# A two-layer graph network on one core: when GpSimd issues its adding transfers, and what the last batch does once attention is over

## The chip, the cores and the metric

The kernel runs on one core of a Trainium2 chip. The metric is the time of one execution on the device, in microseconds (us), as the median of the runs. A core has five engines with a queue of instructions each: TensorE (PE, with its weight loads as PEld), VectorE (DVE), ScalarE (ACT), GpSimd (POOL) and SyncE (SP, which here only issues transfers), and 16 DMA engines that move data for all of them.

## The reference

There are B = 16 batches of N = 1024 nodes with D = 256 features, and a 0/1 matrix `adj` of 1024 x 1024 per batch. Cut to what matters, each batch computes this:

```python
h = relu(layernorm(x))
v = layernorm(h) * gamma1 + beta1              # 8 heads of 32, queries = keys = values
h = h + softmax(where(adj > 0, v v^T / sqrt(32), -inf)) v            # per head
x = x + h + gelu(layernorm2(h) @ W1 + b1) @ W2 + b2                  # W1: 256 x 1024
f = relu(layernorm(x))
hh = f @ W
e = leaky_relu(hh a_1 (as a row) + hh a_2 + (hh a_12) hh^T)
x = x + elu(f @ W_1 + (softmax(where(adj > 0, e, -9e15)) f) @ W_2)
```

The kernel takes softmax without subtracting a row's maximum. At the end it tests that this was harmless: that all denominators of the second softmax (`dens`) lie in a range, and that the sum of squares of the folded weights is under 1e4. If not, a general program (`general_path`) would compute everything again. The test's result is `redo`.

## The kernel before

`fast_path` writes out all 16 batches as one straight program. Nothing loops on the chip; the order is decided when the program is written.

**Attention of a batch** (`attention`, stream A) has 32 units: 2 halves of the queries (`qh`), 2 groups of 4 heads (`g`), 8 tiles of 128 keys (`kt`). A unit makes scores `s` on TensorE (L937), adds the mask on VectorE into two tiles `e`, one for each pair of heads (L958; the first pair is "half 0", the second "half 1"), and takes their exponential on ScalarE (L961). One unit later `weigh` multiplies them with the values into `o` (L974). For the denominators the exponentials of the 8 key tiles are added up: the two tiles of `kt` = 0 are the sums `acc`, and each later tile is added to its `acc` by a transfer that adds on its way (L999, `add_up`), issued on GpSimd's queue. A transfer adds to what the last transfer of the same half has left, so it waits until that one has landed. In batch 0 only the even `kt` are added in this way. After the eighth tile, `go_on` takes a finished group in three steps, one per unit: `weigh`, then a step in which it lies in `summed`, then `total`, which multiplies `acc` with ones (`den`, L888). `finish` follows as an entry of the list `turns`: it transposes denominators and sums (`ptds`, `ptos`, L909), divides, and adds to `h`. The tiles `e` come from a pool of five (`ep`).

**The rest of a batch** (`rest`, stream B) runs beside the attention of the next batch: four chunks of 256 nodes go through `expand` (`ph`, W1, gelu) and `contract` (`po`, W2), then the second layer: `project` (`puT`), `values` (`pg`), `weights` (`lg`), `attend` (`pf`, `pa`). Ahead of each stage lies a normalization: `norm_stats` takes mean and variance on VectorE (L705 to L708) and the power -1/2 on GpSimd (`rs`, L710); VectorE then scales (`y`, `ft`, L714); TensorE transposes (`pty` L1095, `ptf` L1171). The last two `attend` of a batch (`tail`) are run inside the `rest` of the next batch; after the last batch they end the program.

**The order** comes from a planner. Each stream is a Python generator that yields a place (batch number plus fraction) after each piece, and the stream with the lowest place goes next. A piece of stream B moves its place on by its estimated time over 134 us; a unit of attention moves stream A's by 1/32. Two side lists shift work: `turns` holds transposes that wait for the next unit of attention (`ask` appends, `make_turns` empties), and `defer(us, f)` holds work that is written out when the planner's `clock` has advanced by `us`. The clock is a plan, not a measured time: `go_on` adds 2.0 per unit, most pieces of stream B add 1.75. Each engine keeps the order in which its instructions were written out. GpSimd's queue so holds, in one order, the adding transfers, the powers `rs`, the products for the values (`nrm`, `va`, L780 and L781), the sums of the residuals (`h`, `xb`, L1067 and L1068) and the addition of `finish` (L916).

**The end.** After the last unit `close_attention` calls `go_on` four times to empty those three steps, with places between 16 and 16.05. It then sets `quarters[0] = False`: from there matmuls of the rest are written as whole 128-column ones (L567) and not as four of 32 columns (L570). Once stream A has ended, `turns` is emptied only when stream B says that it can't go on (`wait_for`, which yields `0.0, None`). After the last output the test is made: L1433 to L1441 reduce `dens` and the folded weights to `seen` on VectorE, a matmul with ones adds over the partitions (`pn`, L1443), and L1445 to L1448 make `redo`, which all engines load.

The lines that set when a transfer is written out, and what empties the list at the end:

```python
        def add_up(qh, g, kt, es):                                   # L995
            if b == 0 and kt % 2:
                return
            for e, a in zip(es, sums[g, qh]):
                nc.gpsimd.dma_start(a, e, accum_op=ALU.add)
...
                defer(1.5, lambda u=u, es=es: add_up(*u, es))        # L1011
...
                    if places[1] is None:                            # L1380
                        make_turns()
```

Of the kernel before, what the change touches and what calls it, by code (L numbers as in the profile page):

```python
# [16 lines left out]
P = 128  # L17
# [476 lines left out]
def fast_path(  # L494
# [158 lines left out]
    nc.gpsimd.memset(gw[:, :, D + 1 : D + 2], 1.0)  # L653
    dens = const.tile([P, B * NT], F32, name="dens")

    def setup():
        wl, wa, wT, wb = (lp1.tile([P, DC, D], F32, tag="e1", name=f"stage_{i}") for i in range(4))
        weights_to_load.extend([(wl, W), (wa, a_12)])  # L660
        for t, src in rows_to_load:
            nc.sync.dma_start(t, src)
        for t, src in weights_to_load:
            nc.scalar.dma_start(t, src.rearrange("(c p) n -> p c n", p=P))
        yield

        for oc in range(DC):
            pt = ps_tile([P, DC, P], f"p_wT_{oc}")
            for ic in range(DC):
                nc.tensor.transpose(pt[:, ic, :], wl[:, ic, oc * P : (oc + 1) * P], ident)  # L670
            nc.scalar.copy(wT[:, oc, :], pt.rearrange("p c q -> p (c q)"))
        clock[0] += 0.5
        yield

        def product(dst, lhs, rhs, n, name):

            for oc in range(DC):
                pp = ps_tile([P, n], f"p_{name}_{oc}")
                for kc in range(DC):
                    matmul(  # L680
                        pp,
                        lhs[:, kc, oc * P : (oc + 1) * P],
                        rhs[:, kc, :n],
                        start=(kc == 0),
                        stop=(kc == DC - 1),
                    )
                nc.scalar.copy(dst[:, oc, :], pp)

        product(wb, wa, wT, D, "wb")
        clock[0] += 1.7  # L690
        yield
        product(wm, wT, wb, D, "wm")
        product(w_a2.unsqueeze(2), wT, a2c.unsqueeze(2), 1, "w_a2")
        product(wo2[:, :, D : D + 1], wT, a1c.unsqueeze(2), 1, "w_a1")
        nc.gpsimd.memset(wo2[:, :, D + 1 : D + 2], 0.0)
        clock[0] += 2.0
        yield

    def norm_stats(srcs, name):
# [218 lines left out]
    def attention(b, st):  # L918
        va, kT = st["va"], st["kT"]


        def scores(qh, g, kt):
            qs = slice(qh * QW, (qh + 1) * QW)
            sc = [
                psc.tile([P, 2, QW], F32, tag=f"sc{i}", name=f"s_{b}_{g}_{qh}_{kt}_{i}") for i in range(2)
            ]

            by_pe = 2 if b == 0 else 0
            if by_pe:
                for j in range(by_pe):  # L930
                    matmul(
                        sc[j // 2][:, j % 2, :], ident8, st[qh][:, kt // 2, :, kt % 2], start=True, stop=False
                    )
                clock[0] += 0.45
            for j in range(GH):
                r = slice(j * HD, (j + 1) * HD)
                nc.tensor.matmul(  # L937
                    sc[j // 2][:, j % 2, :],
                    kT[r, g, kt * P : (kt + 1) * P],
                    kT[r, g, qs],  # L940
                    start=j >= by_pe,
                    stop=True,
                )
            mb = st[qh][:, kt // 2, :, kt % 2].unsqueeze(1).to_broadcast([P, 2, QW])
            es = []
            if b == 0 and kt % 2:

                odd = midp.tile([P, 2, 2, QW], F32, tag="mid", name=f"odd_{g}_{qh}_{kt}")
            for i in range(2):
                if b == 0 and kt % 2:  # L950
                    e = odd[:, i]
                elif kt == 0:
                    e = accp.tile([P, 2, QW], F32, tag=f"acc{i}", name=f"acc_{b}_{g}_{qh}_{i}")
                else:
                    e = ep.tile([P, 2, QW], F32, tag="e", name=f"e_{b}_{g}_{qh}_{kt}_{i}")
                masked = sc[i]
                if 2 * i >= by_pe:
                    nc.vector.tensor_tensor(e, masked, mb, op=ALU.add)  # L958
                    masked = e
                es.append(e)  # L960
                weights = lambda e=e, masked=masked: nc.scalar.activation(e, masked, AF.Exp, scale=SCALE)  # L961
                if i == 0:
                    weights()
            return es, weights

        acc = {}


        def weigh(qh, g, kt, es):
            if kt == 0:  # L970
                acc[g, qh] = pso.tile([P, QW], F32, tag="o", name=f"o_{b}_{g}_{qh}")
            o = acc[g, qh]
            for j in range(GH):
                nc.tensor.matmul(  # L974
                    o[j * HD : (j + 1) * HD, :],
                    va[:, kt, (g * GH + j) * HD : (g * GH + j + 1) * HD],
                    es[j // 2][:, j % 2, :],
                    start=(kt == 0),
                    stop=(kt == NT - 1),
                )  # L980
            if b == 0 and kt % 2:

                if kt > 1:
                    for n, (e, w) in enumerate(zip(es, odds[g, qh])):
                        defer(1.0 + 2.5 * n, lambda e=e, w=w: nc.vector.tensor_add(e, e, w))
                odds[g, qh] = es
            if kt == NT - 1:
                c = tmpp.tile([P, QW], F32, tag="w2", bufs=3, name=f"os_{b}_{g}_{qh}")
                nc.vector.tensor_copy(c, o)
                weighed.append((b, qh, g, c, [s[g, qh] for s in (sums, odds) if s]))  # L990

        sums, odds = {}, {}


        def add_up(qh, g, kt, es):  # L995
            if b == 0 and kt % 2:
                return
            for e, a in zip(es, sums[g, qh]):
                nc.gpsimd.dma_start(a, e, accum_op=ALU.add)  # L999

        units = [(qh, g, kt) for qh in range(NQH) for g in range(NG) for kt in range(NT)]
        for u in units:
            make_turns()
            es, rest_of_weights = scores(*u)
            go_on()
            rest_of_weights()
            qh, g, kt = u
            if kt == 0:
                sums[g, qh] = es
            else:  # L1010
                defer(1.5, lambda u=u, es=es: add_up(*u, es))  # L1011
            scored.append((weigh, (*u, es)))
            yield

# [24 lines left out]
    def prepare(b, st, c):  # L1039
# [11 lines left out]

        st["y", c] = None, defer(5.0, apply)

    def rest(b, st, tails):

        h = hs[b]
# [16 lines left out]
        def ask(turn, c):  # L1073

            def f():
                clock[0] += 0.5
                turn(c)
                turned.add((turn, c))
            turns.append((1, f))

        def wait_for(turn, c):
            while (turn, c) not in turned:
# [160 lines left out]
        def attend(t, es):  # L1243
# [27 lines left out]
                nc.sync.dma_start(rows(out, b, t), z)  # L1271

            defer(1.0, lambda: nc.scalar.activation(en, z, AF.Exp, bias=ones[:, 0:1]))
            defer(6.0, store)
            yield 1.75, True

# [70 lines left out]
            before = es  # L1347

        def tail():
            for i in range(TPC):  # L1350
                yield from attend((NCH - 1) * TPC + i, before)

# [13 lines left out]
    def stream_a():  # L1366
        for b in range(B):
            yield from spread(attention(b, states[b]), 32, b, b + 1)
        yield from spread(close_attention(), 4, B, B + 0.05)

    def stream_b():
        for b in range(B):
# [55 lines left out]

    good = ep.tile([P, B * NT], F32, tag="e", name="good")
    nc.vector.tensor_scalar(good, dens, DEN_MIN, None, op0=ALU.is_ge)  # L1433
    nc.vector.scalar_tensor_tensor(good, dens, DEN_MAX, good, op0=ALU.is_le, op1=ALU.mult)
    seen = smallp.tile([P, 2], F32, tag="seen", name="seen")
    nc.vector.tensor_reduce(seen[:, 0:1], good, axis=mybir.AxisListType.X, op=ALU.add)
    sq = ep.tile([P, DC * D + 2 * DC], F32, tag="e", name="sq")
    for src, o, n in ((wm, 0, DC * D), (w_a2, DC * D, DC), (wo2[:, :, D], DC * D + DC, DC)):
        src = src.rearrange("p c n -> p (c n)") if len(src.shape) == 3 else src
        nc.vector.tensor_tensor(sq[:, o : o + n], src, src, op=ALU.mult)  # L1440
    nc.vector.tensor_reduce(seen[:, 1:2], sq, axis=mybir.AxisListType.X, op=ALU.add)  # L1441
    pn = ps_tile([1, 2], "pn")
    nc.tensor.matmul(pn, ones[:, 0:1], seen, start=True, stop=True)  # L1443
    fit = smallp.tile([1, 2], F32, tag="fit", name="fit")
    nc.vector.tensor_scalar(fit[:, 0:1], pn[:, 0:1], float(P * B * NT), None, op0=ALU.is_ge)  # L1445
    nc.vector.tensor_scalar(fit[:, 1:2], pn[:, 1:2], 1.0e4, None, op0=ALU.is_le)
    nc.vector.tensor_mul(fit[:, 0:1], fit[:, 0:1], fit[:, 1:2])
    nc.vector.tensor_scalar(redo, fit[:, 0:1], -1.0, 1.0, op0=ALU.mult, op1=ALU.add)  # L1448

    last = {}  # L1450
# [74 lines left out]
```

## Time and profile before

| what | value |
|---|---|
| time, median of 3 runs | 3539.3 us (3532.96 to 3562.22) |
| the profiled run | 3545.29 us, span of its instructions 3543.5 us |
| TensorE busy | 3458.9 us (98%) |
| VectorE / ScalarE / GpSimd busy | 77% / 52% / 40% |
| adding transfers | 864 of 512 KB, 453.04 MB, 69.8% of the DMA engines' span |

A line of a group or of the timeline names engine, source line and operation, then "out<-in" by the program's own names; "x8" is a number of instructions, and "[1.53 <-DVE xb L1149]" says that the engine stood idle for 1.53 us ahead of it and that this instruction ended the wait. The records of matmuls overlap, and their ends are modelled, so that TensorE's busy share also covers short gaps. "PEclk" is the clock granted to TensorE as a share of the full one.

### The profile page before, as it was taken

What the parts mean: (1) busy time and instruction counts of PE and PEld (TensorE: products, weight loads), DVE (VectorE), ACT (ScalarE), POOL (GpSimd) and SP (SyncE); (2) the same over time, 40 slices, a digit from 0 to 9 for tenths busy, and PEclk for the clock granted to TensorE, in tenths of its full rate; (3) what the DMA queues carried; (4) which work ended last, traced back from release to release, by engine and by line L of the source; (5) the groups of instructions that cost most, each with busy time, mean ns of one, the idle gap of its engine ahead of it and who ended that gap; (6) DMA issues with size and microseconds to landing.
All of it is one profiled execution on the core that took longest, in us unless ns stands there. A gap on an engine that the chain in (4) does not pass through costs nothing.

```text
span 3543.5 us, 107149 instructions
## 1 busy us (share of the span) xinstructions
PE 3458.9 (98%) x46494; PEld 1674.4 (47%) x46494; DVE 2733.4 (77%) x5189; ACT 1854.2 (52%) x2184; POOL 1414.0 (40%) x1708
## 2 busy tenths in 40 slices
PE   6999999999999999999999999999999999999998
PEld 2344444444444444444444444444444444444467
DVE  6878787787787877878787787877878778787744
ACT  5655554455555555555555555555555555555522
POOL 3543443434434344453434434344343444533220
PEclk9999999999999999999999999999999999999999
DMA  7799989999899998989989988998999989899710
GB/s 186 157 177 176 188 164 175 169 180 179 160 188 171 185 186 165 186 167 182 188 171 183 170 181 180 185 181 157 187 168 182 188 161 188 170 182 179 153 40 14
DMA packets 281859, 597.79 MB, mean 169 GB/s; under 512 B 94882, under 2 KB 130084, under 8 KB 281380
## 3 DMA queue, kind: packets, MB, share of 16 engines
q0 software_dynamic: 124416, 453.04, 69.8%
q1 hardware_dynamic: 154276, 134.41, 15.1%
q8 instruction: 367, 6.01, 0.7%
q10 hardware_dynamic: 2688, 3.41, 0.3%
q14 instruction: 112, 0.92, 0.1%
HBM read 104.21 MB, written 16.78 MB: 34 GB/s over the span
## 4 chain that ended last, share of the span: by engine, by line
PE 73%; DMA 13%; DVE 5%; issue 5%; POOL 2%; ACT 2%; ACTq 0%; SPq 0%; POOLq 0%; DVEq 0%
PE s L937 12%; DMA acc<-e 12%; PE pa L570 11%; PE o L974 10%; PE lg L570 10%; PE ph L570 9%; PE po L570 7%; PE pf L570 3%; PE pg L570 2%; DVE e L958 2%; PE puT L570 2%; PE den L888 1%; PE ptk L788 1%; PE pa L567 1%; POOL acc L999 1%
## 5 line engine op out<-in xcount | busy, mean ns | idle before, releaser
L961 ACT ACTIVATE e<-e 128x1024 f32<-128x1024 f32 x852 | 895.4, 1057 | 1011.8 <-DVE e L958 776.3
L999 POOL DMA_DIRECT2D acc<-e x864 | 759.2, 885 | 1664.4 <-ACT e L961 710.3
L958 DVE TENSOR_TENSOR e<-s,mk 128x1024 f32<-128x1024 f32 x852 | 1002.5, 1216 | 183.6 <-PE s L937 150.1
L937 PE MATMUL s<-kT 32*128 32x512 f32 x4096 | 596.4, 644 | 4.8 <-DVE e L958 2.7
L974 PE MATMUL o<-e,va 128*32 128x512 f32 x3456 | 463.2, 606 | 2.1 <-ACT e L961 2.1
L570 PE MATMUL ph<-yT,w 128*32 128x256 f32 x7808 | 450.0, 380 | 0.0
L570 PE MATMUL lg<-fT,uT 128*32 128x256 f32 x7680 | 448.6, 380 | 0.0
L570 PE MATMUL pa<-gw,e 128*32 128x258 f32 x7552 | 446.5, 380 | 0.0
L570 PE MATMUL po<-w,hid 128*32 128x256 f32 x7680 | 439.0, 379 | 0.0
L570 PEld LDWEIGHTS ph<-yT,w 128*32 128x32 f32 x7808 | 254.7, 110 | 215.6 <-issue 54.1
L570 PEld LDWEIGHTS lg<-fT,uT 128*32 128x32 f32 x7680 | 249.7, 110 | 211.1 <-issue 44.9
L570 PEld LDWEIGHTS po<-w,hid 128*32 128x32 f32 x7680 | 250.0, 110 | 209.2 <-issue 59.1
L570 PEld LDWEIGHTS pa<-gw,e 128*32 128x32 f32 x7552 | 244.7, 110 | 210.3 <-issue 56.8
L1219 DVE SCALAR_TENSOR_TENSOR e<-lg,gw,mk 128x256 f32<-128x256 f32 x512 | 223.0, 477 | 73.8 <-PE lg L570 63.4
L1225 ACT ACTIVATE e<-e,shift 128x512 f32<-128x512 f32 x256 | 182.2, 717 | 176.3 <-DVE e L1224 110.4
L1122 DVE TENSOR_TENSOR hid<-ph,b1c 128x512 f32<-128x512 f32 x256 | 175.1, 686 | 95.3 <-PE ph L570 81.4
L937 PEld LDWEIGHTS s<-kT 32*128 32x128 f32 x4096 | 163.8, 184 | 165.7 <-issue 114.2
L974 PEld LDWEIGHTS o<-e,va 128*32 128x32 f32 x3456 | 68.8, 108 | 332.5 <-issue 191.9
L961 ACT ACTIVATE acc<-acc 128x1024 f32<-128x1024 f32 x124 | 130.5, 1057 | 125.6 <-DVE acc L958 121.5
L1224 DVE SCALAR_TENSOR_TENSOR e<-e 128x512 f32<-128x512 f32 x256 | 188.7, 737 | 8.8
L958 DVE TENSOR_TENSOR acc<-s,mk 128x1024 f32<-128x1024 f32 x124 | 146.0, 1217 | 16.6 <-PE s L937 16.2
L1129 ACT ACTIVATE hid<-hid 128x2048 f32<-128x2048 f32 x64 | 122.3, 1911 | 36.0 <-DVE hid L1122 35.3
(144 smaller groups left out, 3822.7 us busy)
## 6 DMA issues: line engine op xcount, KB each, us to landing
acc<-e POOLq DMA_DIRECT2D x864, 512.0 KB, 6.0
adj<-in_adj_dram SPq DMA_DIRECT2D x248, 256.0 KB, 5.2
h<-in_x_dram SPq DMA_DIRECT2D x64, 256.0 KB, 6.3
xb<-in_x_dram SPq DMA_DIRECT2D x128, 128.0 KB, 5.3
out_dram<-z SPq DMA_DIRECT2D x128, 128.0 KB, 3.7
adj<-in_adj_dram SPq DMA_DIRECT2D x4, 512.0 KB, 6.7
mk<-mq SPq DMA_TRANSPOSE x128, 6.5
w<-in_L_gnn_W_dram ACTq DMA_DIRECT2D x2, 1024.0 KB
```

The source lines that it names most:

```text
L567: nc.tensor.matmul(out, lhsT, rhs, start=start, stop=stop)
L570: nc.tensor.matmul(out[c : c + HD], lhsT[:, c : c + HD], rhs, start=start, stop=stop)
L937: nc.tensor.matmul(sc[j // 2][:, j % 2, :], kT[r, g, kt * P : (kt + 1) * P], kT[r, g, qs], start=j >= by_pe, stop=True,)
L958: nc.vector.tensor_tensor(e, masked, mb, op=ALU.add)
L961: weights = lambda e=e, masked=masked: nc.scalar.activation(e, masked, AF.Exp, scale=SCALE)
L974: nc.tensor.matmul(o[j * HD : (j + 1) * HD, :], va[:, kt, (g * GH + j) * HD : (g * GH + j + 1) * HD], es[j // 2][:, j % 2, :], start=(kt = ...
L999: nc.gpsimd.dma_start(a, e, accum_op=ALU.add)
L1122: nc.vector.tensor_tensor(hid[:, f0 : f0 + 2, :], ph, b1c[:, f0 : f0 + 2].unsqueeze(2).to_broadcast([P, 2, CW]), op=ALU.add,)
L1129: return hid, defer(1.0, lambda: nc.scalar.activation(hid, hid, AF.Gelu))
L1219: nc.vector.scalar_tensor_tensor(e[:, j, :], lg[:, j, :], gw[:, kt, D : D + 1], st[c // 2][:, kt // 2, qs, kt % 2], op0=ALU.add, op1=ALU.add,)
L1224: nc.vector.scalar_tensor_tensor(e, e, ALPHA, e, op0=ALU.mult, op1=ALU.max)
L1225: ready = defer(2.5, lambda: nc.scalar.activation(e, e, AF.Exp, bias=shift))
```

## The change

There are four edits, of which the fourth has three places.

1. The adding transfers of a unit are written out one by one: half 0 after 2.0 on the planner's clock, half 1 after 3.5. Before, both came after 1.5.
2. `ask` empties `turns` at once when `quarters[0]` is False, that is, after the end of attention.
3. `close_attention` spreads its four calls over places 16 to 16.1.
4. The sums of the last test: those over the folded weights move into a fifth piece of `setup` in batch 0; those over `dens` are taken in two parts, columns 0 to 125 at the start of the last `tail` and the last two columns right after the last denominator is read. `seen` has four columns, and one more reduction adds them in pairs.

```diff
+    seen = const.tile([P, 4], F32, name="seen")
...
+        sq = lp1.tile([P, DC * D], F32, tag="e1", name="sq")
+        few = smallp.tile([P, 2 * DC], F32, tag="few", bufs=1, name="few")
+        wmf = wm.rearrange("p c n -> p (c n)")
+        nc.vector.tensor_tensor(sq, wmf, wmf, op=ALU.mult)
+        nc.vector.tensor_tensor(few[:, :DC], w_a2, w_a2, op=ALU.mult)
+        nc.vector.tensor_tensor(few[:, DC:], wo2[:, :, D], wo2[:, :, D], op=ALU.mult)
+        nc.vector.tensor_reduce(seen[:, 0:1], sq, axis=mybir.AxisListType.X, op=ALU.add)
+        nc.vector.tensor_reduce(seen[:, 1:2], few, axis=mybir.AxisListType.X, op=ALU.add)
...
-        def add_up(qh, g, kt, es):
+        def add_up(qh, g, kt, e, i):
             if b == 0 and kt % 2:
                 return
-            for e, a in zip(es, sums[g, qh]):
-                nc.gpsimd.dma_start(a, e, accum_op=ALU.add)
+            nc.gpsimd.dma_start(sums[g, qh][i], e, accum_op=ALU.add)
...
-                defer(1.5, lambda u=u, es=es: add_up(*u, es))
+                for i in range(2):
+                    defer(2.0 + 1.5 * i, lambda u=u, e=es[i], i=i: add_up(*u, e, i))
...
+    def count_fit(lo, hi, i):
+        good = smallp.tile([P, hi - lo], F32, tag=f"good{i}", bufs=1, name=f"good_{i}")
+        nc.vector.tensor_scalar(good, dens[:, lo:hi], DEN_MIN, None, op0=ALU.is_ge)
+        nc.vector.scalar_tensor_tensor(good, dens[:, lo:hi], DEN_MAX, good, op0=ALU.is_le, op1=ALU.mult)
+        nc.vector.tensor_reduce(seen[:, i : i + 1], good, axis=mybir.AxisListType.X, op=ALU.add)
...
             turns.append((1, f))
+            if not quarters[0]:
+                make_turns()
...
+            if n == B * NT - 1:
+                count_fit(n + 1 - TPC, n + 1, 3)
...
         def tail():
+            if b == B - 1:
+                count_fit(0, B * NT - TPC, 2)
...
-        yield from spread(close_attention(), 4, B, B + 0.05)
+        yield from spread(close_attention(), 4, B, B + .1)
...
-    good = ep.tile([P, B * NT], F32, tag="e", name="good")
-    nc.vector.tensor_scalar(good, dens, DEN_MIN, None, op0=ALU.is_ge)
...
-    pn = ps_tile([1, 2], "pn")
+    pn = ps_tile([1, 4], "pn")
     nc.tensor.matmul(pn, ones[:, 0:1], seen, start=True, stop=True)
     fit = smallp.tile([1, 2], F32, tag="fit", name="fit")
...
+    nc.vector.tensor_reduce(fit, pn.rearrange("o (i j) -> o i j", j=2), axis=mybir.AxisListType.X, op=ALU.add)
+    nc.vector.tensor_scalar(fit[:, 0:1], fit[:, 0:1], 1.0e4, None, op0=ALU.is_le)
+    nc.vector.scalar_tensor_tensor(
+        fit[:, 0:1], fit[:, 1:2], float(P * B * NT), fit[:, 0:1], op0=ALU.is_ge, op1=ALU.mult
+    )
     nc.vector.tensor_scalar(redo, fit[:, 0:1], -1.0, 1.0, op0=ALU.mult, op1=ALU.add)
```

More of the change, by code (lines that the diff above doesn't have):

```diff
@@ L696, in setup @@
         clock[0] += 2.0
+        yield
+        sq = lp1.tile([P, DC * D], F32, tag="e1", name="sq")
[6 more added lines that the diff above has]
+        nc.vector.tensor_reduce(seen[:, 1:2], few, axis=mybir.AxisListType.X, op=ALU.add)
         yield
@@ L1427, in fast_path @@
     run_deferred()
-    good = ep.tile([P, B * NT], F32, tag="e", name="good")
-    nc.vector.tensor_scalar(good, dens, DEN_MIN, None, op0=ALU.is_ge)
[L1434 to L1441, printed above, removed]
-    pn = ps_tile([1, 2], "pn")
+    pn = ps_tile([1, 4], "pn")
     nc.tensor.matmul(pn, ones[:, 0:1], seen, start=True, stop=True)
     fit = smallp.tile([1, 2], F32, tag="fit", name="fit")
-    nc.vector.tensor_scalar(fit[:, 0:1], pn[:, 0:1], float(P * B * NT), None, op0=ALU.is_ge)
-    nc.vector.tensor_scalar(fit[:, 1:2], pn[:, 1:2], 1.0e4, None, op0=ALU.is_le)
-    nc.vector.tensor_mul(fit[:, 0:1], fit[:, 0:1], fit[:, 1:2])
+    nc.vector.tensor_reduce(fit, pn.rearrange("o (i j) -> o i j", j=2), axis=mybir.AxisListType.X, op=ALU.add)
[3 more added lines that the diff above has]
+    )
     nc.vector.tensor_scalar(redo, fit[:, 0:1], -1.0, 1.0, op0=ALU.mult, op1=ALU.add)
```

## The prediction

> **What bounds the kernel now.** I read the page's head first, then its chain of work, then the windows by stage, the waits, and at last the timeline where TensorE waited.
>
> ```profile
> span 3543.5 us, 107149 instructions
> PE 3458.9 (98%) x46494; PEld 1674.4 (47%) x46494; DVE 2733.4 (77%) x5189; ACT 1854.2 (52%) x2184; POOL 1414.0 (40%) x1708
> ...
> PE 73%; DMA 13%; DVE 5%; issue 5%; POOL 2%; ACT 2%; ACTq 0%; SPq 0%; POOLq 0%; DVEq 0%
> ...
> acc<-e POOLq DMA_DIRECT2D x864, 512.0 KB, 6.0
> ```
>
> TensorE bounds it: busy for 98%, 73% of the chain. The chain's second part, 13%, is the adding transfers; each takes 6.0 us to land, in a unit of attention of about 6.7 us (215 us a batch over 32 units). They are the near second. So only what makes TensorE wait can be won, and the windows say how much there is (columns: length, busy PE, PEld, DVE, ACT, POOL, granted clock, DMA share, GB/s):
>
> ```profile
> 0.00:230.00 230.00, 192.62 (x2080) 73.34 (x2084) 173.63 (x311) 124.77 (x142) 101.79 (x131) 1.00 0.81 175
> 230.00:3360.00 3130.00, 3103.24 (x43480) 1472.77 (x43476) 2471.45 (x4670) 1681.60 (x1978) 1290.92 (x1551) 1.00 0.90 176
> 3360.00:3543.50 183.50, 163.06 (x946) 128.32 (x938) 88.29 (x210) 47.87 (x66) 21.26 (x28) 0.96 0.14 32
> 569.70:576.60 6.90, 6.90 (x42) 2.28 (x44) 4.93 (x10) 3.98 (x5) 1.72 (x2) 0.51 1.03 220
> 3378.90:3385.70 6.80, 5.61 (x52) 2.36 (x54) 0.23 (x1) 0.58 (x1) 0.00 (x0) 0.50 0.02 4
> ```
>
> In 15 batches' body TensorE is idle for 3130.0 - 3103.2 = 26.8 us, at the end for 183.5 - 163.1 = 20.4 us. The last two rows show a second price: after a wait of 2.7 us the clock is at half for some 6.9 us, which costs about 3.4 us more. Two more such stretches, of 3.4 us each, follow at 689 and 2409 us. Half of 6.9 + 3.4 + 3.4 makes 6.9 us in the body, so that at most 26.8 + 6.9 = 34 us can be won there.
>
> ```profile
> POOL acc L999 <- ACT e L961: 710.3, 274, 9.8
> POOL acc L999 <- DMA acc<-e: 655.2, 288, 8.0
> ...
> DVE ft L714 <- POOL rs_d L710: 59.1, 26, 5.1
> ...
> DVE y L714 <- POOL rs_c L710: 19.9, 13, 5.2
> ```
>
> These are waits: total us, times, longest. GpSimd's queue stands for 655.2 us with an adding transfer at its head that waits for the landing of the one before, and for 710.3 us with one that waits for its exponential. What stands behind it waits too: VectorE lost 59.1 + 19.9 us to the powers `rs_d` and `rs_c`. One case on three engines:
>
> ```profile
> 898.77 0.86 POOL L999 DMA_DIRECT2D acc<-e  x1 [1.65 <-DMA acc<-e]
> ...
> 900.02 1.01 POOL L710 TENSOR_TENSOR rs_d<-ve_d,mhalf 128x2 f32<-128x2 f32 x1
> ...
> 901.06 0.74 DVE L714 TENSOR_SCALAR ft<-xb,mv_d,rs_d 128x256 f32<-128x256 f32 x2 [3.69 <-POOL rs_d L710]
> ...
> 904.62 0.41 DVE L1149 TENSOR_TENSOR xb<-po,xb 128x256 f32<-128x256 f32 x1
> ...
> 905.09 1.08 PE L570 MATMUL pg<-wo,fT 128*32 128x258 f32 x16 [1.53 <-DVE xb L1149]
> ```
>
> Transfer, power, scaling, then the sum `xb` that frees a PSUM buffer, then TensorE: 1.5 us lost. The end has three waits of its own:
>
> ```profile
> 3380.09 1.07 PE L888 MATMUL den<-acc,ones 128*32 128x512 f32 x2 [2.69 <-DMA acc<-e]
> ...
> 3400.76 7.14 PE L567 MATMUL ph<-yT,w 128*128 128x256 f32 x32 [3.20 <-DVE yT L1099]
> ...
> 3536.80 0.19 PE L1443 MATMUL pn<-seen,ones 128*1 128x2 f32 x2 [4.96 <-DVE seen L1441]
> ```
>
> **What the Trainium skill says.** "DMA: Bandwidth & Descriptors", section "SWDGE vs HWDGE vs iDMA", says that adding during a transfer can be issued by GpSimd only; section "Two DMAs through the same engine are not ordered" has the issuing engine wait for the first transfer's semaphore. So neither queue nor wait can be given up, and the 288 waits above agree. "TensorE: Matmul & The Clock Gate", section "Part 1: The HAM clock gate", gives half clock after an idle window of about 3.4 us; here 2.7 us at 3380 were enough, though 3.2 us at 3400 had no such stretch, so I count it only where the trace has it. The same page ("Architectural detail: the array is 16× 32×32, not 1× 128×128") calls GpSimd's queue first in, first out, as the example shows.
>
> **Edit 1, transfers later.** No instruction is added or removed: 864 transfers of 0.86 us on GpSimd. Between two units stream B writes 134/32 = 4.2 us of pieces, mostly two or three of 1.75. So 1.5 was due after the first piece, 2.0 comes after the second, and 3.5 after the second, the third or the next unit. Powers, value products and residual sums of one or two pieces now pass ahead of the transfers; none falls behind. In the example stream B writes the normalization that holds `rs_d` with the second piece: both transfers of that unit then come after it, and `rs_d` runs when its variance is ready. I count 14 us of the 34, between none and all: about two fifths, as part of the waits is another's (`puT` waits for ScalarE's copies, `ptos` for VectorE).
> The transfers pay. A half-0 transfer can stand behind a power that waits for VectorE, 1 to 2 us. Who waits for it: VectorE's `e` two units later, which reuses the buffer (10.8 us in 9 waits now), and `den`. From the landings and the 64 starts of `den`, half 1 lands 6.0 us ahead at the median, and under 2.6 us ahead in one group of twenty: a delay under 2 us is mostly hidden. In batch 0, with no stream B, the clock gains 2.45 a unit, so half 1 comes after two units; I take 1 us of loss there (0 to 5). SP's queue isn't touched.
>
> **Edits 2 and 3, the end.** TensorE's order follows from the places. `den` now comes after four pieces `ph` and not two, 2 x 1.73 = 3.5 us later; its waits of 0.65 + 2.69 = 3.3 us vanish but for some 0.9 us, and with them the half clock, 3.4 us: 5.8 us. The transpose `pty` of chunk 1 is done between two halves of `attend` and not after both, so `yT` is ready: 3.2 us. `pty` of chunks 2 and 3 comes ahead of 6.9 us of `po`: 2 x 0.64 = 1.3 us. The transposes `ptf` likewise: 0.3 + 0.8 = 1.1 us. The later `finish` has 1.7 us of `pa` and 6.9 us of `ph` to hide its chain (0.25 + 0.69 + 1.27 + 1.4 + 0.7 + 0.73 = 5.0 us): nothing. Sum 11.4 us (7 to 13).
>
> **Edit 4, the test.** From the end of the last `pa` (3531.86) to `redo` (3537.60) lie 5.7 us. What remains: three operations to `z` (1.0), three counts on two columns at about 0.2 (0.6), the stores' four operations (1.7), four small ones at about 0.17 (0.7): 4.0, so 1.8 us less (1.0 to 2.3). The loads and branches behind it, 5.9 us, stay, and hide the output transfer of 3.7 us, which is issued 0.6 us later. Added: 0.8 us on VectorE at the last `tail`, where it waits 2.0 us for `pa` anyway; 0.68 + 2 x 0.15 + 0.69 + 0.15 = 1.8 us in batch 0, where VectorE is busy for 84% of that stretch: 0 to 1.8, I take 0.5, as its releasers there are ScalarE and the transfers as often.
>
> **Sum.** 14 - 1 + 11.4 + 1.8 - 0.5 = 25.7 us of the profiled span, 3543.5 to 3518. That run took 3545.3 us, above the median of 3539.3; from the median it is 3539.3 - 25.7 = 3514.
>
> **Rivals.**
> *Only the end gains* (30%): the blocked powers wait behind the next transfer instead. For it: the queue still has 864 transfers that wait for landings, DMA share 0.90. Against: no transfer moves forward. 3539.3 - 13 = 3526.
> *The whole body clears* (15%): all 34 us go. For it: nearly all long waits at batch ends lead to `rs`. Against: those on ScalarE remain. 3539.3 - 34 - 13 = 3492.
> *Transfers too late, slower* (6%): each unit's half 1 waits behind a power that waits for VectorE (9.8 us at the longest), the delay adds up over seven tiles, since 6.0 us of landing leave only 0.7 us a unit to catch up, and `den` waits. It decides once half 1 lands more than 6 us later at the 60 groups: at 7 us, 60 x 1 = 60 us, 3539.3 + 60 - 13 = 3586.
> *The edits don't do it* (7%): the end's waits move to `finish`, the body stays: 3538.
>
> **How the numbers follow.** My forecast has 42%, with 3503 to 3524 of its own. The range is 3490 to 3541: it leaves out the late transfers and the lower part of the cleared body. One per cent, 35 us, is about what a measurement of this kernel can tell from no change (its runs spread over 29 us). Faster than 3504: the cleared body and some of mine, 0.27; slower 0.06; the rest 0.67.
>
> **What would show it.** VectorE's waits for `rs_d` and `rs_c` fall from 79 us to under 30; the idle time of the body to about 15 us; half-clock stretches in the body from three to one or none; no wait for `yT` over 0.3 us at the end and no half clock at 3380; `pn` waits under 4 us. GpSimd's waits for landings may stay. Wrong would be: waits of `den` or of `e` for transfers of over 20 us in all, or `rs` waits that stay.

## The result, and the profile after

The changed kernel takes 3501.56 us (median of 4 runs, 3501.38 to 3501.71), beside 3538.23 us (3532.96 to 3562.22) for the kernel before. The ratio is 0.9879, with a 95% interval of 0.9848 to 0.991. The profiled span went from 3543.5 to 3499.6 us, 43.9 us less, where the prediction's sum had 25.7.

To see where, I cut each trace by TensorE's score matmuls, of which every unit of attention has the same number: batch 0 reaches from its first unit to that of batch 1, the body from there to the last unit of batch 15, the end from there to the end of the span.

| stage, us | before | after | difference | predicted |
|---|---|---|---|---|
| up to the first unit | 25.8 | 25.9 | +0.1 | 0 |
| batch 0 | 124.9 | 130.0 | +5.1 | +1.5 |
| body | 3215.1 | 3178.7 | -36.4 | -14 |
| end | 177.7 | 165.0 | -12.7 | -13.2 |

In the body 12 of the 14 batches with a successor, all but batches 1 and 10, last 212.7 to 212.9 us each after the change; before they lie between 210.0 and 219.7, without a pattern.

The page of the changed kernel: its head, the shares of the chain that ended last, and the adding transfers with their size and median time to landing.

```profile
span 3499.6 us, 107320 instructions
PE 3445.0 (98%) x46590; PEld 1673.9 (48%) x46590; DVE 2758.3 (79%) x5193; ACT 1857.8 (53%) x2184; POOL 1412.8 (40%) x1708
...
PE 94%; DVE 3%; DMA 1%; issue 1%; ACT 0%; POOL 0%; ACTq 0%; SPq 0%; DVEq 0%; POOLq 0%
...
acc<-e POOLq DMA_DIRECT2D x864, 512.0 KB, 6.1
```

TensorE's share of the chain went from 73 to 94%, that of the transfers from 13 to 1%. The transfers themselves are no faster: the same number, the same size, a landing of 6.1 instead of 6.0 us. They have only left the path. The windows of the changed kernel (length, then busy PE, PEld, DVE, ACT, POOL, then granted clock, DMA share, GB/s) give the rest:

```profile
230.00:3360.00 3130.00, 3126.06 (x44022) 1494.52 (x44011) 2520.55 (x4719) 1701.71 (x1997) 1303.16 (x1565) 1.00 0.91 178
3320.00:3499.60 179.60, 168.29 (x1178) 129.94 (x1170) 95.10 (x227) 54.50 (x74) 24.78 (x33) 0.99 0.18 42
85.20:88.60 3.40, 3.11 (x20) 0.71 (x17) 3.30 (x7) 2.90 (x4) 1.55 (x2) 0.50 0.94 222
95.40:102.20 6.80, 6.25 (x36) 1.80 (x39) 5.64 (x12) 3.52 (x4) 1.19 (x3) 0.50 0.68 128
```

TensorE is idle for 3.9 us of these 3130, where it was 26.8 us before. The last two rows are as much as batch 0 lost: 3.4 + 6.8 us at half clock (their granted clock is 0.50), which cost about half of that, 5.1 us. In the profile of the kernel before, batch 0 has no such stretch, and the body has 6.8 + 3.4 + 3.4 us; after, the body has none. So 22.9 us of the body's 36.4 are idle time that went, 6.8 us are half clock that went, and 6.7 us appear in neither view; where they went is not shown (the ends of matmuls are modelled, so that a short wait may look busy).

What TensorE waited for between 230 and 3310 us (engine and operation, who released it: total us, times, longest). Before:

```profile
PE pg L570 <- DVE xb L1149: 7.5, 5, 2.5
PE ptf L1171 <- DVE ft L714: 7.3, 8, 1.6
PE ptos L909 <- DVE e L1219: 3.4, 14, 0.2
PE s L937 <- DVE e L958: 2.7, 1, 2.7
PE puT L570 <- ACT gw L1201: 2.2, 5, 1.0
PE ptf L1171 <- ACT uT L1186: 1.5, 6, 0.3
PE pg L570 <- ACT uT L1186: 0.3, 1, 0.3
PE ptos L909 <- DVE hid L1122: 0.3, 1, 0.3
```

After, in the same stretch, this one line is the whole answer:

```profile
PE ptos L922 <- DVE e L1241: 3.4, 14, 0.2
```

The waits put down to VectorE's `xb`, `ft` and `e` and to ScalarE's `gw` and `uT` went together, though edit 1 (the only edit that touches the body after batch 0) changed the order of GpSimd's queue only. What that queue waited for after the change, over the whole span:

```profile
POOL acc L1011 <- DMA acc<-e: 637.3, 289, 6.2
POOL acc L1011 <- ACT e L974: 447.1, 189, 9.8
...
POOL rs_a L723 <- DVE ve_a L721: 157.1, 53, 12.4
```

The queue stands as often as before with a transfer at its head that waits for a landing (288 times before), but for an exponential 189 times, not 274. The power `rs_a` waits for its variance for 157.1 us instead of 55.1: GpSimd now reaches the power before VectorE has its input, so the power no longer comes late. No wait of VectorE for `rs_c` or `rs_d` is left.

TensorE's timeline at the end, after (start, length, what; in brackets the idle time and who ended it):

```profile
3347.74 1.03 PE L901 MATMUL den<-acc,ones 128*32 128x512 f32 x4
3349.29 0.62 PE L901 MATMUL den<-acc,ones 128*32 128x512 f32 x2 [0.52 <-DMA acc<-e]
...
3360.63 7.07 PE L567 MATMUL ph<-yT,w 128*128 128x256 f32 x32
3367.96 0.78 PE L1117 MATMUL pty<-ident,y 128*128 128x128 f32 x4 [0.27 <-DVE y L727]
...
3416.33 0.67 PE L1193 MATMUL ptf<-ident,ft 128*128 128x128 f32 x4 [0.93 <-DVE ft L727]
```

`den` waits 0.5 us here, with no half clock behind it; `ph` starts without a wait where it had 3.20 us. In turn `pty` and `ptf` wait 0.27 and 0.93 us, as transposes that run at once meet operands that have just been written.

### The profile page after: what moved, and what is told of

Read it like the earlier page. It is cut to its first block, busy times and chain, and to the rows that moved or that the text cites. A ratio compares the mean times of both kernels' runs of the same rounds, so it can differ in the third digit from the quotient of the medians.

```text
span 3499.6 us, 107320 instructions
## 1 busy us (share of the span) xinstructions
PE 3445.0 (98%) x46590; PEld 1673.9 (48%) x46590; DVE 2758.3 (79%) x5193; ACT 1857.8 (53%) x2184; POOL 1412.8 (40%) x1708
## 4 chain that ended last, share of the span: by engine, by line
PE 94%; DVE 3%; DMA 1%; issue 1%; ACT 0%; POOL 0%; ACTq 0%; SPq 0%; DVEq 0%; POOLq 0%
PE s L950 15%; PE o L987 13%; PE pa L570 12%; PE po L570 12%; PE ph L570 12%; PE lg L570 10%; PE pg L570 3%; PE pf L570 3%; PE puT L570 3%; PE den L901 2%; PE ptf L1193 1%; PE pty L1117 1%; PE ptk L801 1%; PE ptos L922 1%; PE pa L567 1%
## 5 line engine op out<-in xcount | busy, mean ns | idle before, releaser
L793 POOL TENSOR_TENSOR nrm<-nrm,g 128x256 f32<-128x256 f32 x128 | 112.9, 882 | 63.8 <-DVE nrm L727 63.8
```

The lines of the kernel that those rows point to most:

```text
L793: nc.gpsimd.tensor_mul(nrm, nrm, g1)
```

## The experiments

The kernel before ran again beside each group of these kernels; its medians there were 3549 to 3551 us and single runs 3531 to 3569 us. So for its variants I give the stages of the profile and, where several runs were made, the ratio. A profile is one execution, and the stages are its stages: for "powers off GpSimd" and "powers and products off" it is the longest of 20 and of 4 runs (3549.2 and 3527.2 us), so that their bodies probably lie above what is usual for them. The idle time is that of TensorE between 230 and 3330 us, from the windows of each profile.

| run | batch 0 | body | end | body idle | median us |
|---|---|---|---|---|---|
| before | 124.9 | 3215.1 | 177.7 | 26.8 | 3538 to 3551 |
| before, again | 126.8 | 3208.0 | 177.9 | 22.6 | 3540.3 (one run) |
| edit 1 alone | 131.5 | 3181.5 | 176.6 | 3.6 | 3517.2 |
| both halves at 2.0 | 126.6 | 3181.8 | 165.6 | 4.1 | 3505.1 |
| only half 1 later | 129.5 | 3191.0 | 164.8 | 10.5 | 3520.4 |
| later still | 133.6 | 3182.0 | 170.7 | 3.4 | 3519.0 |
| before's places in batch 0 | 131.6 | 3178.1 | 164.7 | 4.4 | 3504.0 |
| powers off GpSimd | 131.6 | 3210.6 | 179.3 | 25.6 | 3539.0 |
| powers and products off | 124.2 | 3198.4 | 178.6 | 14.2 | 3521.0 |
| the same, six buffers | 125.2 | 3185.4 | 179.9 | 8.5 | 3515.4 |
| edits 2 and 3 | 124.4 | 3226.4 | 167.2 | 31.8 | 3540.8 |
| edit 2 alone | 125.9 | 3215.6 | 169.4 | 26.0 | 3538.4 (one run) |
| edit 4 alone | 126.6 | 3241.0 | 176.3 | 42.9 | 3571.4 (one run) |
| after | 130.0 | 3178.7 | 165.0 | 3.4 | 3501.6 |

**Which edit.** Edit 1 alone, in the kernel before:

```
-                defer(1.5, lambda u=u, es=es: add_up(*u, es))
+                for i in range(2):
+                    defer(2.0 + 1.5 * i, lambda u=u, e=es[i], i=i: add_up(*u, e, i))
```

> The kernel before with edit 1 alone (transfers half by half, after 2.0 and 3.5). I cut the span in three stages by the first score matmul of a unit of attention: batch 0 (before 124.9 us, changed 130.0), batches 1 to 15 up to their last unit (3215.1 and 3178.7), and the end from that unit on (177.7 and 165.0). If the transfers alone make the body faster: body 3179 to 3182 us, end 176 to 178, about 3510 us in all. If the body's gain came from elsewhere in the change: body 3210 to 3220. If the later transfers cost batch 0 its 5 us, batch 0 is 129 to 131 here; if the sums moved into it do, 125.

Ratio 0.989 (0.9844 to 0.9936). The body is 3181.5 us, 2.8 above that of the whole change, and the end is hardly moved. So the body's gain is edit 1's.

Edit 4 alone, the sums of the test in batch 0 and at the last `tail`, with the transfers, the transposes and the last places as before:

> The kernel before with edit 4 alone (the sums of the last test early). End 177.7 - 1.8 = 175.9 us, by the changed kernel's redo, which comes 3.6 us after the last pa and not 5.7. Batch 0: 125 to 125.5 us if the 1.8 us of sums on VectorE are hidden, 127 if not, 130 if they cause the half-clock stretches there.

Its end is 1.4 us shorter. Its total, 3571.4 us, lies above every run of the kernel before, and its body, 3241.0 us, above the other profiles of the old order (3208 to 3226). From one run I can't tell whether the edit costs the old order something. In the changed kernel no such loss is seen: its body is no longer than that of edit 1 alone.

**Batch 0.** The changed kernel with the transfers of batch 0 at their old place:

```
-                    defer(2.0 + 1.5 * i, lambda u=u, e=es[i], i=i: add_up(*u, e, i))
+                    defer(2.0 + 1.5 * i if b else 1.5, lambda u=u, e=es[i], i=i: add_up(*u, e, i))
```

> The changed kernel, but in batch 0 both transfers come after 1.5 as before. If half 1 after two units is what cost batch 0 its 5 us: batch 0 back at 125 to 126 us, no half-clock stretch at 85 and 95 us, 3496 to 3497 us in all, faster than both kernels. If the sums in setup cost it: batch 0 stays at 129 to 130, 3501 us in all.

Batch 0 took 131.6 us, as slow as with the later transfers, so they are not its loss. The clock is: this run has 3.4 + 6.8 + 3.4 us at half clock there, and 131.6 less half of these 13.6 us is 124.8; after the change it is 130.0 - 5.1 = 124.9, as before. One wait for a later transfer is in the trace all the same: `den` waits 1.38 us in batch 0 after the change, and not at all with the old places there. The stage less its half clock doesn't show it. The kernel before, unchanged, once more:

> The kernel before once more, unchanged, for the spread of its stages between executions. If batch 0 differs by run and not by kernel: between 124 and 132 us, not 124.9 again within 1 us. If it is the kernel: 124.9 within 1 us, and the change's 130.0 is a loss of its own. The body 3205 to 3245 us.

126.8 us, so the first case: batch 0 differs by run. It has 6.8 us at half clock, and 123.4 us without their cost. The two executions of this one kernel have the same wait in batch 0. In the first and in the second:

```profile
93.24 0.61 PE L570 MATMUL s<-mk,ident 128*32 128x512 fp8e5 x8 [2.71 <-ACT acc L961]
```

```profile
94.44 1.04 PE L570 MATMUL s<-mk,ident 128*32 128x512 fp8e5 x8 [2.71 <-ACT acc L961]
```

In the first the clock stays full there; in the second it is at half from 93.8 to 100.6 us, and the same 8 matmuls take 1.04 us and not 0.61. All runs but two lie at 121.5 to 124.9 us by this reckoning. The two are edit 1 alone, 126.4, and the run with still later transfers, 130.2. Whether the change makes the stretches in batch 0 more frequent stays open: the kernel before has 0 and 6.8 us of them, edit 1 alone 10.2, but the old places with the powers off GpSimd (below) have 17.0.

**Why edit 1 helps: the powers.** The prediction blamed powers that stand behind blocked transfers. So I took the powers off GpSimd's queue and left the transfers where they were. A reciprocal on VectorE stands in for the power:

```
-        nc.gpsimd.tensor_tensor(rs, ve, mhalf[:, :nt], op=ALU.pow)
+        nc.vector.reciprocal(rs, ve)
```

> The kernel before, transfers as before, but the powers are taken off GpSimd's queue: each rs is a reciprocal on VectorE in place of a power -1/2 on GpSimd, so the normalizations divide by the variance and not by its root, and the output is not the reference's. Theory 'the powers waited behind blocked transfers': the body falls most of the way, to 3180 to 3195 us, though the transfers' own timing is as before. Rival 'the transfers' own times are what helps (they are spread, and collide less with each other and with loads)': the body stays at 3210 to 3220 us or gets longer by VectorE's 256 added instructions.

The ratio is 0.9964 (0.995 to 0.9978): the median is 11.8 us shorter, where edit 1 alone gave 33.6 us beside the same runs of the kernel before. The profiled run, the longest of the 20, has a body of 3210.6 us, within the spread of the old order. No wait for a power is left in it, and the two waits of TensorE that the prediction traced back to powers, for `xb` (7.5 us) and for `ft` (7.3 us), are gone. But TensorE is idle as long as before, since others took their place: for `ds` 5.0 us, `e` 4.8, `gw` 3.1, `ptos` 6.6 in place of 3.4. Part of this can be VectorE's added reciprocals. Two waits of other engines that grew, between 230 and 3330 us:

```profile
DVE e L958 <- DMA acc<-e: 37.7, 27, 4.9
ACT h L767 <- POOL va L781: 21.3, 7, 3.5
```

They were 10.8 and 3.4 us. ScalarE waits for the value product `va`, which stands in the same queue behind the same transfers, and VectorE waits for the landing that frees a buffer of `e`. With the first cause removed, the next ones in line showed, and a part of the gain was had.

**The value products too.** Beside the powers, the two operations of the value product leave the queue; VectorE writes the normalized rows straight into `va`, without their scaling:

```
-                normalize(nrm, h[t // TPH][:, t % TPH, :], mv, rs, j)
-                nc.gpsimd.tensor_mul(nrm, nrm, g1)
-                nc.gpsimd.tensor_add(va[:, t, :], nrm, be1)
+                normalize(va[:, t, :], h[t // TPH][:, t % TPH, :], mv, rs, j)
```

> Leaves out of the kernel before the powers (a reciprocal on VectorE instead) and the scaling by g1 and adding of be1 of the value product, so that GpSimd's queue holds only the transfers, placed as before, and the residual sums. Theory A (what costs the body is any computing on GpSimd that stands behind a blocked transfer, powers and value products alike): body from the first unit of batch 1 to the last unit near 3182 us, as with edit 1, and no wait of ScalarE for va. Rival B (the cost lies in the transfers' own places: buffers of e come free too late, and VectorE's exponents wait for landings): body stays near 3210 us and VectorE's waits of e for landings stay near 38 us. End stage as before, 178 us.

Ratio 0.9912 (0.9886 to 0.9938); body 3198.4 us, 10 below the lowest profile of the old order, idle time 14.2 us. Between the two expectations: half the idle time has gone with the blocked computing, and the waits for landings stayed, as the rival had it. VectorE's wait for landings in this kernel, between 230 and 3330 us, and TensorE's for what VectorE then writes late:

```profile
DVE e L955 <- DMA acc<-e: 33.9, 18, 5.4
...
PE s L934 <- DVE e L955: 7.3, 4, 2.8
```

**Six buffers.** The same kernel with a sixth buffer for `e`, which tells whether the waits for landings are what was left. The constants `g1` and `be1`, unused in it, go as well, to make room:

```
-    ep = pool("ep", 5)
+    ep = pool("ep", 6)
```

> The kernel of e9_clear (powers and value products off GpSimd, transfers placed as before) with six instead of five buffers for the exponents e. If what was left of the body's loss there is VectorE waiting for a landed transfer before it may write the next e: those waits fall from 33.9 us to under 5 us, and the body from 3198 to 3180-3187 us. If it is the residual sums still on GpSimd, or another wait: the body stays at 3193 us or more.

VectorE's wait for landings in this kernel, in the same stretch of 230 to 3330 us:

```profile
DVE e L953 <- DMA acc<-e: 3.4, 3, 1.2
```

The wait fell to 3.4 us and the body to 3185.4, both as the first theory had it, and TensorE no longer waits for `e`. The medians of these two kernels, 3521.0 and 3515.4 us, differ by less than the profiles' bodies do (5.6 against 13.0 us; the first of the profiles is of that kernel's longest run), and their ratios' intervals overlap; the waits are the firmer reading. The two ran on different chips, on which the kernel before took 3549.0 and 3549.7 us. What is idle still, 8.5 us, is mostly `ptos`, 6.4 us, which VectorE's added work may delay (3.4 in the kernel before).

So two things cost the body its time: computing that stood in GpSimd's queue behind blocked transfers, and buffers of `e` that came free late. In medians, taking the powers off gave 11.8 us, the products too 27.9, the sixth buffer too 34.3, and edit 1 alone 33.6. In the kernel before, the second cause reached TensorE only once (2.7 us, with 6.8 us of half clock); it grew when the first was taken away. Edit 1 removes both with neither of these means. VectorE's waits of `e` for landings between 230 and 3330 us, in the kernel before and after the change:

```profile
DVE e L958 <- DMA acc<-e: 10.8, 9, 2.7
```

```profile
DVE e L971 <- DMA acc<-e: 1.6, 1, 1.6
```

That the first cause goes follows from the order. The second was a surprise, as every transfer is written out later. The trace shows what went with it. The time to landing (least, median, longest) of the adding transfers in the kernel before, from the view of their line:

```profile
DMA to landing us min/median/max: 4.5/6.0/13.7
```

The same of its mask transposes `mk<-mq` on SP's queue, from the view of their tile:

```profile
DMA to landing us min/median/max: 2.4/6.5/14.2
```

The adding transfers after the change:

```profile
DMA to landing us min/median/max: 4.5/6.1/11.5
```

And the mask transposes after it:

```profile
DMA to landing us min/median/max: 2.4/6.5/9.4
```

The medians stay, the longest landings shrink, of both kinds together. Between 150 and 3330 us, 25 adding transfers before took over 9.5 us, and 9 after; the profiles with the transfers at 1.5 have 21 to 36, those at 2.0 or later for both halves 5 to 14. The two profiles without powers and products on GpSimd have 32 and 28, so it is the transfers' own places that matter here, and not the computing in their queue. All of the 25 and 8 of the 9 are in flight with a mask transpose or a mask load; of all adding transfers in that stretch 343 of 827 are before, and 361 of 838 after. So the late ones are among those that meet a mask's transfers, but after the change as many meet them. Why fewer of these then land late was not shown: no run moved the mask's transfers.

**How late, and which half.** Both halves at 2.0 in the changed kernel:

```
-                    defer(2.0 + 1.5 * i, lambda u=u, e=es[i], i=i: add_up(*u, e, i))
+                    defer(2.0, lambda u=u, e=es[i], i=i: add_up(*u, e, i))
```

> The changed kernel with both halves' transfers at 2.0. Theory A (the first half step, past the second piece of the other stream, is what lets computing pass ahead): body within 5 us of the changed kernel, 3179 to 3184 us, total 3500 to 3507 us. Rival B (the split matters: the second half's transfer must come late, or the first half's waits stand in front of it): body 3190 to 3205 us, total 3512 to 3528 us.

The ratio is 0.9875 (0.9854 to 0.9896), that of the change itself. By the planner's clock 2.0 is past the second piece, so passing it is what counts, and not the split by halves. With half 0 at 1.5 and half 1 at 3.5 (`1.5 + 2.0 * i`):

> The changed kernel with half 0's transfer at 1.5 as before and half 1's at 3.5. If it is half 1's transfer alone that blocks, because it waits for the later exponential: body 3179 to 3184 us. If half 0's, ahead of it in the queue and waiting for the same unit's exponentials, blocks as much: body 3195 to 3210 us. Theory A gives the second: half 0's transfer at 1.5 stands ahead of the same computing.

Body 3191.0 us, idle 10.5 us: two thirds of the gain, between the two cases. Half 0 alone at the old place still costs a third of the gain; half 1 alone there was not tried. Both still later, at 3.5 and 5.0 (`3.5 + 1.5 * i`):

> The changed kernel with the transfers at 3.5 and 5.0 instead of 2.0 and 3.5. Theory (the gain is had once the computing of the second piece passes ahead, and later is only worse): body 3185 to 3200 us with waits of e for landings over 10 us, and den waits at the tiles' ends, total 3510 to 3530 us. Rival (the later the better): body at or under 3178 us, total 3498 to 3502 us. The rival of the record that late transfers end on the slow side would show over 3560 us.

The body, 3182.0 us, was better than the theory's 3185 to 3200, with hardly a wait of `e` for a landing in it (2.3 us): it has room for at least 1.5 more on the planner's clock. The loss came where nothing hides a landing. TensorE's wait in this kernel, over the whole span:

```profile
PE den L901 <- DMA acc<-e: 7.5, 5, 3.3
```

In batch 0 and at the last tile `den` waits for the transfer, with half clock behind it: batch 0 is 3.6 us longer and the end 5.7 us longer than after the change. The median is 3519.0 us, the range of the theory, for other reasons than it gave.

**The end.** Edits 2 and 3 alone:

```
+            if not quarters[0]:
+                make_turns()
...
-        yield from spread(close_attention(), 4, B, B + 0.05)
+        yield from spread(close_attention(), 4, B, B + .1)
```

> Edits 2 and 3 alone. End stage, from the last unit of attention to the end, 166 us against 177.7 before: no half clock at den, no wait for yT, as the prediction's 11.4 us have it. Rival (the waits move to the other pieces): 173 to 178 us. The body stays that of before, 3205 to 3245 us.

The end is 167.2 us, 10.5 shorter, with the body that of the old order. No half clock follows `den`, in this profile or in the four others that have edits 2 and 3 and no transfer later than 3.5; in all seven with the old end it does, for 3.4 or 6.8 us. Edit 2 alone:

> Edit 2 alone, the transposes made at once when no attention is left. By the prediction's terms (3.2 us for yT, 1.3 for the transposes of y, 1.1 for those of ft) the end stage is 177.7 - 5.6 = 172 us, and the half clock at den stays. If TensorE's order there needs edit 3 as well: 176 to 178 us. Body as before, and it varies by run.

169.4 us, 8.3 shorter, more than expected, and for a reason that isn't the edit's. The timeline of this kernel at `den`:

```profile
3377.81 1.05 PE L888 MATMUL den<-acc,ones 128*32 128x512 f32 x4 [0.69 <-DMA acc<-e]
3381.22 0.62 PE L888 MATMUL den<-acc,ones 128*32 128x512 f32 x2 [2.36 <-DMA acc<-e]
```

`den` waits as it did before (0.65 and 2.69 us), but in this execution no half clock follows: the second row's matmuls take 0.62 us, and 1.07 in the kernel before. Without those 3.4 us the edit's part is 8.3 - 3.4 = 4.9 us.

## Why the prediction was right, and where it was off

The predicted time, 3514 us, is 12.4 us too high; the measured one lies in its range, though not in the likeliest case's own range of 3503 to 3524, and was closest to the rival of the cleared body (3492). The range of 3490 to 3541 was wide enough for three of the four rivals too, so lying in it says little of the mechanism; the stages and the waits say more.

- **TensorE is the bound, and only its waits can be won.** Right: the body now runs at TensorE's pace, with 3.9 us of idle time in 3130 us.
- **Edit 1, the body: predicted 14 of at most 34 us, measured 36.4.** This is the term that was mis-sized. The step that failed is "about two fifths, as part of the waits is another's (`puT` waits for ScalarE's copies, `ptos` for VectorE)". The two waits that it names come to 2.2 + 3.4 us, which leaves far more than two fifths; no other working stands behind that share. And the releaser named in the last link was taken for the cause. The waits of `puT`, `pg`, `ptf` and `s` all went with a change of GpSimd's order; only `ptos` was of another kind, and stays at 3.4 us. The mechanism was right as far as it went: with the powers off the queue the waits for `xb` and `ft` went. But it was too narrow: that gave 11.8 us in the median, about a third of what edit 1 gave, and the rest lay with value products in the same queue and with the buffers of `e`. Even the bound of 34 us was too low: 36.4 us were won, with 3.9 us of idle time left.
- **"The transfers pay": half right.** `e` and `den` were named as the ones to wait for late landings. In the body the waits of `e` fell to 1.6 us, and the longest landings became shorter with them. Over the 64 groups half 1 lands 3.9 us ahead of its `den` at the median, 6.0 before, and in the body that is enough. `den` pays 1.38 us in batch 0; batch 0 and the end pay more when the transfers come later still.
- **Batch 0: predicted 1 + 0.5, measured 5.1.** The reason given, half 1 coming after two units, is seen in `den`'s 1.38 us, but it isn't the loss: with the old places in batch 0 the stage was no shorter. The loss is 10.2 us at half clock, which the sum left out for this stage.
- **Edits 2 and 3: predicted 11.4, measured 10.5 by themselves.** By part, `yT`, `pty` and `ptf` were to give 5.6 us and gave about 4.9 (edit 2 alone, less the half clock that stayed away by itself); edit 3 adds 2.2 us, beside the half clock where it occurs.
- **Edit 4: predicted 1.8, measured 1.4 alone, and 167.2 - 165.0 = 2.2 on top of edits 2 and 3, there together with edit 1.** `pn` now waits for this long, where it was 4.96 us:

```profile
3491.41 0.19 PE L1458 MATMUL pn<-seen,ones 128*1 128x4 f32 x2 [1.59 <-DVE seen L1072]
```

- **The rivals.** "Only the end gains" fell with edit 1 alone. "The whole body clears" is what the body did; against it I had held the waits on ScalarE. "Transfers too late" needed landings later by over 6 us at all 60 groups; even with 1.5 more on the planner's clock the body keeps its gain. "The edits don't do it" fell in both stages.

## What to carry to other kernels

Where an engine's queue mixes waiting transfers with short computing, count what stands behind the transfers, and price the waits of every engine downstream, not those alone whose last releaser is on that queue: here they vanished together. Moving a transfer past the computing was cheap as long as its landing had slack; look for the places without it, here batch 0 and the last tile. To tell causes apart, take away one kind of work from the queue at a time and watch which wait takes its place.

## What the runs showed of the hardware

- Half clock comes in stretches of 3.4 or 6.8 us, and not after every like wait. `den`'s 0.65 + 2.69 us and 1.88 + 1.85 us (the kernel before, twice) were followed by 6.8 us of it, 0.69 + 2.36 us (edit 2 alone) by none. The wait of `ph` at the end was followed by none in the kernel before (3.20 us, both times), by 3.4 us of it with edit 4 alone (3.20 us too) and with six buffers (3.39 us). The same 32 matmuls, in the kernel before and in the one with six buffers:

```profile
3400.76 7.14 PE L567 MATMUL ph<-yT,w 128*128 128x256 f32 x32 [3.20 <-DVE yT L1099]
```

```profile
3369.09 8.83 PE L567 MATMUL ph<-yT,w 128*128 128x256 f32 x32 [3.39 <-DVE yT L1094]
```

They took 1.7 us more with a stretch of 3.4 us, half of it. The Trainium skill, "TensorE: Matmul & The Clock Gate", section "Part 1: The HAM clock gate", says that the activity window of about 3.4 us is free-running and its effect differs between runs; the lengths agree. Its idle window of about 3.4 us is longer than these waits, and there the measurement decides.
- The runs of the old order spread more: 29 us over 4 runs of the kernel before, 0.3 us over 4 runs after, with nearly the same matmuls to do. The 0.3 is in part luck, as 4 runs of edit 1 alone spread over 7.8 us, and 4 with the old places in batch 0 over 7.3 us. What makes the spread was not tested.
- Adding transfers of 512 KB keep a median landing of 6.0 to 6.1 us in both kernels at a DMA share of 0.90 to 0.91 in the body, while their longest goes from 13.7 to 11.5 us (11.1 us with edit 1 alone, which only shifts their issue).
